# A mixer's gate projections as 2x2 block products with seven multiplications, their output products placed between the halves, and two scalings on another engine

## The chip, the cores and the metric

One core of one Trainium2 chip (trn2). The metric is the device time of one execution in microseconds (us). Three runs of the kernel before took 2802.63, 2804.25 and 2805.12 us; the median is 2804.25.

The core's engines run side by side, each through an instruction list of its own, and meet through semaphores: PE multiplies matrices (PEld is its weight load), DVE, ACT and POOL work on vectors, SP issues the transfers. PE, DVE and ACT meet in PSUM, whose banks hold what PE writes until DVE or ACT have read it; POOL works in SBUF.

## The reference, cut to what matters

A block with cross attention, a state-space mixer and a routed low-rank layer, each on a layer norm and with a residual. x has 8 sequences of 64 tokens and 512 features, 512 tokens in all; everything is fp32. The change lies in the mixer:

```python
proj = einsum('bld,pd->blp', hidden_states, in_proj_w)
gate = proj[..., :I]                       # I = 64 heads * 64 = 4096
hbc  = proj[..., I:I + CONV_DIM]           # x, B and C
dt   = proj[..., -H:]
xBC  = silu(conv over 4 tokens of hbc)
...
y  = scan(xBC, softplus(dt + dt_bias)) + x * D
yn = y * rsqrt(mean of y * y over a group of 512) * norm_weight
yn = yn * silu(gate)
out = einsum('bli,di->bld', yn, out_proj_w)
```

There are 8 groups. Each has 512 gate channels, 512 channels of x, 128 of B and 128 of C, and 8 heads of 64.

## The kernel before, in words

Cross attention takes the first 2303 us and is not touched. It and the queries already use the form of product that the change brings to the gates (`FIRST`, `SECOND` on lines 38 and 39, `weight_sums` on line 137, the queries from line 149): a matrix product is cut into 2x2 blocks, and seven block products of sums of blocks replace eight. In the queries the product is L204, its first copy and sums L220 to L225, the second half's L231 to L233, the sums of weights L141 to L144 on POOL.

`mixer_and_routed` works through the groups. Channels lie on the 128 partitions, the 512 tokens along the free axis. In a group, n counts blocks of 128 channels: n = 0 to 3 are the gates, 4 to 7 x, 8 B and 9 C. `project` (L1112 on) makes one block: four matmuls 128x512 (L1116) into a PSUM bank with the tag `pj`, of which there are three; the output products (`mo`) use the same three. For a gate ACT takes silu from PSUM into `sg` (L1122). For x, B and C, DVE does a convolution over four tokens into `acc` (L1127, then three times L1133), of which there are three buffers, and ACT takes its silu into `xbc` (L1138).

The work of a group is laid over that of its neighbours, in an order written out by hand (from L1289), within which a scheduler places the instructions of each engine by their priority and by `issue_after` (an instruction of the block isn't issued ahead of the one named). In the loop for a group `G`, with `old` the group before and `new` the one after:

- `load_out` fetches the output weights and POOL multiplies them by norm_weight (L1015); `load_in` fetches the next group's input weights; `steps` makes the next group's `av` on POOL (L1089), in four buffers.
- The convolution stretch: projections n = 8, 9, 4, 5, 6, 7, with the mixing of the old group in between: `mix` (products `pg` L1154 and transposes `px` L1165 on PE, `gm` L1158, `m` L1160 and `dx` L1167 on DVE), `scan` (16 small products per 128 tokens, L1183, added into y by DVE, L1189), and `gate` (squares on ACT L1195 and sums of them on POOL L1196 and L1198; y times sg on DVE, L1205). Then `skip`: y = x * D on POOL (L1145).
- ACT loads the table for exp and ln (L116); four sets of `decay` of the new group follow (products `seg` L1104 on PE, exp L1109 on ACT), and `norm` of the old one (`pss` L1211 on PE, then ln and exp on ACT, L1214 and L1215), which gives the factors `rs`.
- The gate stretch: gates n = 0 to 3, each followed by `project_out(old, n)`: four matmuls 128x512 (L1224), then x += product * rs on DVE (L1228).

In the last group the mixing and scans of that same group stand between its gates, and after it come its gate multiplications (L1352), `norm`, the output products and the router. Ahead of the first group stands the softplus of dt (L1035 to L1056), a chain of small instructions on DVE and ACT, on which the first decays wait.

Of the kernel before, what the change touches and what calls it, by code (L numbers as in the profile page):

```python
# [9 lines left out]
F32 = mybir.dt.float32  # L10
AF = mybir.ActivationFunctionType
ALU = mybir.AluOpType
# [3 lines left out]
P = 128  # L16
# [945 lines left out]
def mixer_and_routed(ctx, tc, c, x, done, w_in, w_out, w_ra, b_w, out):  # L962
# [43 lines left out]
    def load_out(G):  # L1006

        g = G.g
        G.wo = wst.tile([P, GC, D], F32, tag="w_out", name=f"w_out_{g}")
        nc.sync.dma_start(  # L1010
            out=G.wo, in_=w_out[g * GC * P : (g + 1) * GC * P, :].rearrange("(n p) o -> p n o", p=P)
        )
        for n in range(GC):
            ct = g * GC + n
            nc.gpsimd.tensor_scalar(G.wo[:, n, :], G.wo[:, n, :], c.nw[:, ct : ct + 1], None, op0=ALU.mult)  # L1015

# [4 lines left out]
    for tt in range(NTT):  # L1021
# [11 lines left out]
    dt = big.tile([P, NTT, H2], F32, name="dt")  # L1033
    z = big.tile([P, NTT, H2], F32, name="sp_z")
    nc.vector.tensor_tensor(z, pdt, c.dtb.unsqueeze(1).to_broadcast([P, NTT, H2]), ALU.add)  # L1035
    e = big.tile([P, NTT, H2], F32, name="sp_e")

    nc.vector.tensor_scalar(dt, z, 0.0, None, op0=ALU.max)
    nc.vector.scalar_tensor_tensor(out=e, in0=dt, scalar=-2.0, in1=z, op0=ALU.mult, op1=ALU.add)
    nc.scalar.activation(e, e, AF.Exp)  # L1040
    u = big.tile([P, NTT, H2], F32, name="sp_u")
    nc.vector.tensor_scalar(u, e, 1.0, None, op0=ALU.add)
    lu = big.tile([P, NTT, H2], F32, name="sp_lu")
    nc.scalar.activation(lu, u, AF.Ln)
# [13 lines left out]
        op0=ALU.mult, op1=ALU.mult,  # L1058
    )


# [21 lines left out]
    def steps(G, tt):  # L1083


        if tt == 0:
            G.av, G.dec = [], grpp.tile([P, NTT, HPG, S], F32, tag="dec", name="dec")
        av = wk.tile([P, 2, HH, S], F32, tag="av", name="av", bufs=4)
        nc.gpsimd.tensor_tensor(  # L1089
            av,  # L1090
            ah[:, :, tt, G.g, :].unsqueeze(3).to_broadcast([P, 2, HH, S]),
            c.upto1.unsqueeze(1).unsqueeze(1).to_broadcast([P, 2, HH, S]),
            ALU.mult,
        )
        G.av.append(av)
# [16 lines left out]
    def project(G, n):  # L1112

        pj = bank("pj", [P, NT], "pj", 3)
        for dc in range(DC):
            nc.tensor.matmul(  # L1116
                pj, lhsT=G.w[:, dc, n, :], rhs=xnT[:, dc, :], start=dc == 0, stop=dc == DC - 1
            )
        if n < GC:
            if n == 0:  # L1120
                G.sg = grpp.tile([P, GC, NT], F32, tag="sg", name="sg")
            return nc.scalar.activation(G.sg[:, n, :], pj, AF.Silu).ins  # L1122
        if n == 8:
# [8 lines left out]
        for k in range(1, KC):  # L1132
# [4 lines left out]
            )  # L1137
        return nc.scalar.activation(G.xbc[:, n - GC, :], acc, AF.Silu).ins  # L1138

    def skip(G):  # L1140

        G.y = grpp.tile([P, GC, NT], F32, tag="y", name="y")
        for n in range(GC):
            ct = G.g * GC + n
            nc.gpsimd.tensor_scalar(G.y[:, n, :], G.xbc[:, n, :], c.dk[:, ct : ct + 1], None, op0=ALU.mult)  # L1145

# [74 lines left out]
    def project_out(G, tt):  # L1221
        po = bank("pj", [P, D], "mo", 3)
        for n in range(GC):
            nc.tensor.matmul(  # L1224
                po, lhsT=G.y[:, n, tt * P : (tt + 1) * P], rhs=G.wo[:, n, :],
                start=n == 0, stop=n == GC - 1,
            )
        nc.vector.scalar_tensor_tensor(  # L1228
            out=x[:, tt, :], in0=po, scalar=G.rs[tt], in1=x[:, tt, :], op0=ALU.mult, op1=ALU.add
        )  # L1230


# [12 lines left out]
    def route(tt):  # L1245
        xnT = wk.tile([P, DC, P], F32, tag="xnT", name="rt_xnT")
        layernorm_T(nc, c, small, ps, x, tt, xnT, tag="px", bufs=2, pbufs=1, copy=nc.scalar.copy)
# [26 lines left out]
        nc.tensor.matmul(po, lhsT=whT, rhs=bw, start=True, stop=True)  # L1274
        o = wk.tile([P, D], F32, tag="o", name="o")
        nc.vector.tensor_tensor(o, x[:, tt, :], po, ALU.add)
# [4 lines left out]
    for tt in range(NTT):  # L1281
        steps(g0, tt)
    last = None
    for tt in range(NTT):
        last = decay(g0, tt)
    for g in range(G2):
# [10 lines left out]
        with tc.issue_after(last):  # L1297

            for n, behind in (
# [8 lines left out]
                if n is not None:  # L1308
                    silus.append(project(G, n))
                if old:  # L1310
                    for what, tt in behind:
                        what(old, tt)
            skip(G)
        with tc.issue_after(silus[-1]):
            table = load_ln_exp(nc).ins
        with tc.issue_after(table):
            if new:
                decay(new, 0)
                decay(new, 1)
        gates = [lambda n=n: project(G, n) for n in range(GC)]  # L1320
        if new:
# [3 lines left out]
        if old:  # L1325
            with tc.issue_after(table):
                last = norm(old, range(NTT))
        with tc.issue_after(last):
            for n in range(GC):
                if not new and n == NTT - 1:  # L1330
                    scan(G, n)
                    squares(G, n)
                last_gate = gates[n]()
                if not new:

                    for tt in ((0, 1), (2,), (3,), ())[n]:
                        mix(G, tt)
                    if 0 < n < NTT - 1:
                        scan(G, n - 1)
                        squares(G, n - 1)  # L1340
                    if n == 2:
                        scan(G, n)
                        squares(G, n)
                if old:
                    project_out(old, n)
        last = last_gate
# [79 lines left out]
```

## Time and profile before

| | us |
|---|---|
| runs | 2802.63, 2804.25, 2805.12 |
| profiled execution | 2806.07 |
| its span | 2804.40 |
| PE, DVE, ACT, POOL busy in the span | 2777.7, 1717.9, 726.3, 837.4 |
| mixer, from its first projection to its last output products | 2308.2 to 2771.6 |
| a middle group, from mixing to mixing (L1154) | 59.35 to 59.6 |
| PE's granted clock, mean | 0.998 of full speed |

How to read it: "busy" is the time in which an engine executes, without semaphores and issue. A line of the timeline gives start, length, engine, line of the kernel, operation, the tile written and those read, the shape, and how many instructions of the kind follow one another; in brackets, idle time ahead of it and what ended it. A row of the groups gives the total time, the mean in ns of one, and the engine's idle time before it with its releaser. In the last line of the page's chain, each engine has the share of the span in which the chain of work that ended last went through it.

### The profile page before, as it was taken

To read this page: it belongs to the slowest core of one execution; us is meant where nothing else is said; L and a number is where in the kernel's file an instruction comes from. 1 tells how busy PE (TensorE), PEld (TensorE's weight loads), DVE (VectorE), ACT (ScalarE), POOL (GpSimd) and SP (SyncE) were. 2 spreads that over 40 slices of the span, in tenths; PEclk is the share of its full clock that TensorE was granted. 3 is DMA by queue.
4 is the path that set the end of the run, shared out by engine and by line. 5 is a ranking of instruction groups with operands and counts; after the bars stand their busy time and mean duration, and the time that the engine had idled before them with its cause. 6 is when DMAs were issued, how large, how long until landed. Compare 5 with 4: busy or idle time off the path is not lost.

```text
span 2804.4 us, 38363 instructions
## 1 busy us (share of the span) xinstructions
PE 2777.7 (99%) x14972; PEld 1980.5 (71%) x14972; DVE 1717.9 (61%) x3044; ACT 726.3 (26%) x1314; POOL 837.4 (30%) x786
## 2 busy tenths in 40 slices
PE   9899999999999999999999999999999999999998
PEld 7677777777777777877777777778777554444444
DVE  4556676566666666765766676667656326444554
ACT  3322223222222322232222222222322103222222
POOL 4313323322222332233222223322322214333431
PEclk9999999999999999999999999999999999999999
DMA  4821322131223213221311232132212541112200
GB/s 156 276 90 46 88 67 55 53 103 44 48 54 90 54 45 89 67 55 52 103 45 48 54 89 54 48 85 67 61 31 80 168 140 38 53 53 86 72 16 15
DMA packets 277230, 206.02 MB, mean 73 GB/s; under 512 B 155676, under 2 KB 240538, under 8 KB 276026
## 3 DMA queue, kind: packets, MB, share of 16 engines
q1 hardware_dynamic: 277050, 203.57, 25.5%
q8 instruction: 119, 1.95, 0.3%
q14 instruction: 61, 0.50, 0.1%
HBM read 180.87 MB, written 22.66 MB: 73 GB/s over the span
## 4 chain that ended last, share of the span: by engine, by line
PE 87%; DVE 3%; ACT 1%; DMA 1%; issue 0%; POOL 0%; SPq 0%; ACTq 0%; DVEq 0%
PE pav L596 13%; PE psc L526 12%; PE pj L1116 8%; PE pv_a L445 6%; PE pv_b L445 6%; PE pk_b L385 6%; PE pv_c L445 6%; PE pk_c L385 6%; PE pk_a L385 5%; PE mo L1224 4%; PE pv_d L445 3%; PE pk_d L385 3%; PE psn L414 2%; DVE acc L1133 1%; PE pvl L468 1%; PE po_d L741 1%
## 5 line engine op out<-in xcount | busy, mean ns | idle before, releaser
L531 DVE SCALAR_TENSOR_TENSOR attn<-psc,rk,mask_sb 128x256 f32<-128x256 f32 (+1 forms) x832 | 364.4, 475 | 190.6 <-PE psc L526 188.8
L580 POOL TENSOR_TENSOR sm<-attn 128x512 f32<-128x512 f32 x64 | 82.0, 1281 | 1196.0 <-ACT attn L578 1196.0
L596 PE MATMUL pav<-attn,v 128*128 128x256 f32 (+1 forms) x1664 | 384.3, 381 | 0.0
L526 PE MATMUL psc<-q,kT 128*128 128x256 f32 x1536 | 367.5, 380 | 0.0
L596 PEld LDWEIGHTS pav<-attn,v 128*128 128x128 f32 (+1 forms) x1664 | 311.1, 190 | 55.4 <-issue 11.1
L583 POOL TENSOR_TENSOR sm<-sm,attn 128x512 f32<-128x512 f32 x256 | 339.9, 1328 | 28.9 <-DVE attn L574 10.6
L526 PEld LDWEIGHTS psc<-q,kT 128*128 128x128 f32 x1536 | 287.5, 190 | 77.1 <-issue 29.9
L1116 PE MATMUL pj<-mx_xnT,w_in 128*128 128x512 f32 x640 | 296.3, 603 | 1.3 <-DVE acc L1133 1.3
L574 DVE TENSOR_TENSOR attn<-attn,nb 128x1024 f32<-128x1024 f32 x192 | 224.7, 1215 | 58.1 <-ACT nb L571 57.3
L445 PEld LDWEIGHTS pv_a<-wv,cx 128*128 128x128 f32 x1536 | 196.0, 191 | 48.2 <-issue 41.4
L578 ACT ACTIVATE attn<-attn 128x1024 f32<-128x1024 f32 x192 | 203.4, 1059 | 79.8 <-DVE attn L574 77.2
L445 PE MATMUL pv_a<-wv,cx 128*128 128x128 f32 x1536 | 213.8, 279 | 0.0
L542 DVE TENSOR_TENSOR mx<-mx,attn 128x512 f32<-128x512 f32 x256 | 212.3, 829 | 2.0
L1116 PEld LDWEIGHTS pj<-mx_xnT,w_in 128*128 128x128 f32 x640 | 115.2, 190 | 129.4 <-issue 124.7
L385 PE MATMUL pk_a<-cx,wk 128*128 128x417 f32 (+1 forms) x512 | 193.3, 500 | 0.8 <-ACT qrs L110 0.8
L396 ACT ACTIVATE ksq<-kT 128x834 f32<-128x834 f32 (+1 forms) x128 | 109.2, 871 | 145.9 <-DVE kT L377 145.9
L385 PEld LDWEIGHTS pk_a<-cx,wk 128*128 128x128 f32 x512 | 97.2, 190 | 46.1 <-issue 20.8
L1228 DVE SCALAR_TENSOR_TENSOR x<-mo,rs,x 128x512 f32<-128x512 f32 x32 | 24.0, 750 | 165.1 <-PE mo L1224 110.4
L1224 PE MATMUL mo<-w_out,y 128*128 128x512 f32 x256 | 118.1, 597 | 0.0
L643 POOL TENSOR_TENSOR o<-o,f 128x512 f32<-128x512 f32 x31 | 40.0, 1291 | 232.7 <-DMA f<-sums_d 199.3
L571 ACT COPY nb<-nbs 128x256 f32<-128x256 f32 x64 | 24.1, 376 | 318.3 <-DMA nbs<-max_d 309.1
L1133 DVE SCALAR_TENSOR_TENSOR acc<-pj,small_consts,acc 128x504 f32<-128x504 f32 (+1 forms) x144 | 103.7, 724 | 0.7
(220 smaller groups left out, 4187.7 us busy)
## 6 DMA issues: line engine op xcount, KB each, us to landing
wk<-in_wk SPq DMA_DIRECT2D x32, 512.0 KB
wv<-in_wv SPq DMA_DIRECT2D x32, 512.0 KB
w_in<-in_w_in SPq DMA_DIRECT2D x16, 1024.0 KB
wvs<-wv_s_d SPq DMA_DIRECT2D x28, 512.0 KB
wks<-wk_s_d SPq DMA_DIRECT2D x28, 512.0 KB
cx<-in_ctxT SPq DMA_DIRECT2D x16, 834.0 KB
cx<-in_ctxT SPq DMA_DIRECT2D x16, 768.0 KB
wq<-in_wq SPq DMA_DIRECT2D x16, 512.0 KB
```

The lines of the kernel that those rows point to most:

```text
L385: nc.tensor.matmul(ps[:, :w], lhsT=u.wk[l][:, dc, :], rhs=u.cx.r[ch][r][:, dc, :], start=start and dc == 0, stop=dc == 1, skip_group_check ...
L445: nc.tensor.matmul(ps[:, i * HD : (i + 1) * HD], lhsT=u.cx.r[ch][r][:, dc, i * P : (i + 1) * P], rhs=u.wv[l][:, dc, :], start=start and i ...
L526: nc.tensor.matmul(ps[:rows, t - t2, :], lhsT=lhsT, rhs=qh, start=True, stop=True)
L531: nc.vector.scalar_tensor_tensor(out=s.at[:rows, t, :].rearrange("p (h q) -> p h q", h=GQ), in0=ps[:rows, t - t2, :].rearrange("p (h q) -> ...
L542: nc.vector.tensor_tensor(s.mx2, s.mx2, s.at[:, t2 : t2 + 2, :], ALU.max)
L574: nc.vector.tensor_tensor(at[:, k : k + 4, :], at[:, k : k + 4, :], nb.unsqueeze(1).to_broadcast([P, 4, 256]), ALU.add,)
L578: nc.scalar.activation(at[:, k : k + 4, :], at[:, k : k + 4, :], AF.Exp)
L583: nc.gpsimd.tensor_tensor(sm2, sm2, at[:, i : i + 2, :], ALU.add)
L596: nc.tensor.matmul(s.av[:, 0, :], lhsT=u.v[:rows, t, hh, :], rhs=s.at[:rows, t, :], start=t == 0, stop=t == NKT - 1,)
L1116: nc.tensor.matmul(pj, lhsT=G.w[:, dc, n, :], rhs=xnT[:, dc, :], start=dc == 0, stop=dc == DC - 1)
L1133: nc.vector.scalar_tensor_tensor(out=accb[:, :, k:], in0=pjb[:, :, : S - k], scalar=c.cw[:, ct, KC - 1 - k : KC - k], in1=accb[:, :, k:], ...
L1224: nc.tensor.matmul(po, lhsT=G.y[:, n, tt * P : (tt + 1) * P], rhs=G.wo[:, n, :], start=n == 0, stop=n == GC - 1,)
```

## The change

1. Gates in pairs of channel blocks (`project_gates`). A pair's product is 256 channels by 512 inputs by 512 tokens, cut in 2x2 blocks. `first` issues four block products (a, d, b, c; two matmuls 128x256 each) into two banks, of which ab holds a and b, cd holds c and d; ACT copies a (p1), DVE makes three sums. `second` issues three more products onto a, b and c, ACT takes silu of a, DVE adds b and c, and ACT takes silu of those. Output products of the old group stand after each half: first, mo0, second, mo1, first, mo2, second, mo3.
2. Sums of weights (`sums_in`, eight per group, POOL, made one group ahead) and, once, sums of tokens (`token_sums`, four 128x512 on DVE).
3. `second` comes after the factors of `norm` (`last`), `first` need not: ACT's first copy may be issued ahead of them.
4. `skip` moves from POOL to ACT, three blocks before the table load, the fourth after the factors. The weighing of the output weights (`weigh_out`) moves from POOL to ACT, after the group's last gate.
5. `behind` is issued after the projection it follows. `av` has three buffers instead of four; the softplus temporaries and two of the router's tiles take other tiles' buffers.

```diff
@@ -1010,9 +1010,19 @@
         nc.sync.dma_start(
             out=G.wo, in_=w_out[g * GC * P : (g + 1) * GC * P, :].rearrange("(n p) o -> p n o", p=P)
         )
+
+    def weigh_out(G):
         for n in range(GC):
-            ct = g * GC + n
-            nc.gpsimd.tensor_scalar(G.wo[:, n, :], G.wo[:, n, :], c.nw[:, ct : ct + 1], None, op0=ALU.mult)
+            ct = G.g * GC + n
+            nc.scalar.activation(G.wo[:, n, :], G.wo[:, n, :], AF.Copy, scale=c.nw[:, ct : ct + 1])
+
+    def sums_in(G, n):
+
+        l = {
+            f"L{k + 1}{e + 1}": G.w[:, 2 * e : 2 * e + 2, n + k, :] for k in range(2) for e in range(2)
+        }
+        G.l = getattr(G, "l", {})
+        G.l[n] = weight_sums(nc, l, wk.tile([P, 4, 2, P], F32, tag="ws", name="ws"))
 
     load_in(groups[0])
 
@@ -1031,16 +1041,17 @@
             )
 
     dt = big.tile([P, NTT, H2], F32, name="dt")
-    z = big.tile([P, NTT, H2], F32, name="sp_z")
+
+    sp = grpp.tile([P, GC, NT], F32, tag="y", name="sp")
+    z, e, u, lu = (
+        sp[:, k, : NTT * H2].rearrange("p (t h) -> p t h", h=H2) for k in range(4)
+    )
     nc.vector.tensor_tensor(z, pdt, c.dtb.unsqueeze(1).to_broadcast([P, NTT, H2]), ALU.add)
-    e = big.tile([P, NTT, H2], F32, name="sp_e")
 
     nc.vector.tensor_scalar(dt, z, 0.0, None, op0=ALU.max)
     nc.vector.scalar_tensor_tensor(out=e, in0=dt, scalar=-2.0, in1=z, op0=ALU.mult, op1=ALU.add)
     nc.scalar.activation(e, e, AF.Exp)
-    u = big.tile([P, NTT, H2], F32, name="sp_u")
     nc.vector.tensor_scalar(u, e, 1.0, None, op0=ALU.add)
-    lu = big.tile([P, NTT, H2], F32, name="sp_lu")
     nc.scalar.activation(lu, u, AF.Ln)
     nc.vector.tensor_scalar(u, u, 1.0, None, op0=ALU.subtract)
     nc.vector.tensor_scalar(z, u, 0.0, None, op0=ALU.is_equal)
@@ -1059,6 +1070,21 @@
     )
 
 
+    HT = NT // 2
+    blocks = {
+        f"R{e + 1}{half + 1}": xnT[:, 2 * e : 2 * e + 2, half * HT : (half + 1) * HT]
+        for e in range(2) for half in range(2)
+    }
+    ts = big.tile([P, 4, 2, HT], F32, name="mx_xs")
+    blocks.update((f"T{k + 1}", ts[:, k]) for k in range(4))
+
+    def token_sums():
+        for o, p, q in (
+            ("T1", "R12", "R11"), ("T2", "R22", "T1"), ("T3", "R22", "R12"), ("T4", "R21", "T2")
+        ):
+            nc.vector.tensor_tensor(blocks[o], blocks[p], blocks[q], ALU.subtract)
+
+
 
     psw = bank("seg", [P, NTT, H2], "psw", 2)
     for r in range(0, P, S):
@@ -1085,7 +1111,7 @@
 
         if tt == 0:
             G.av, G.dec = [], grpp.tile([P, NTT, HPG, S], F32, tag="dec", name="dec")
-        av = wk.tile([P, 2, HH, S], F32, tag="av", name="av", bufs=4)
+        av = wk.tile([P, 2, HH, S], F32, tag="av", name="av", bufs=3)
         nc.gpsimd.tensor_tensor(
             av,
             ah[:, :, tt, G.g, :].unsqueeze(3).to_broadcast([P, 2, HH, S]),
@@ -1113,13 +1139,9 @@
 
         pj = bank("pj", [P, NT], "pj", 3)
         for dc in range(DC):
-            nc.tensor.matmul(
+            done = nc.tensor.matmul(
                 pj, lhsT=G.w[:, dc, n, :], rhs=xnT[:, dc, :], start=dc == 0, stop=dc == DC - 1
-            )
-        if n < GC:
-            if n == 0:
-                G.sg = grpp.tile([P, GC, NT], F32, tag="sg", name="sg")
-            return nc.scalar.activation(G.sg[:, n, :], pj, AF.Silu).ins
+            ).ins
         if n == 8:
             G.xbc = grpp.tile([P, GC + 2, NT], F32, tag="xbc", name="xbc")
         ct = G.g * GC + n - GC if n < 8 else (I2 // P + G.g if n == 8 else I2 // P + G2 + G.g)
@@ -1135,14 +1157,59 @@
                 scalar=c.cw[:, ct, KC - 1 - k : KC - k], in1=accb[:, :, k:],
                 op0=ALU.mult, op1=ALU.add,
             )
-        return nc.scalar.activation(G.xbc[:, n - GC, :], acc, AF.Silu).ins
-
-    def skip(G):
-
-        G.y = grpp.tile([P, GC, NT], F32, tag="y", name="y")
-        for n in range(GC):
+        return done, nc.scalar.activation(G.xbc[:, n - GC, :], acc, AF.Silu).ins
+
+    def project_gates(G, n):
+
+
+
+        st, l = Group(), G.l[n]
+        if n == 0:
+            G.sg = grpp.tile([P, GC, NT], F32, tag="sg", name="sg")
+        to = G.sg[:, n : n + 2]
+
+        def product(k, lhs, rhs, start, stop):
+            for dc in range(2):
+                last = nc.tensor.matmul(
+                    st.ps[k], lhsT=l[lhs][:, dc, :], rhs=blocks[rhs][:, dc, :],
+                    start=start and dc == 0, stop=stop and dc == 1, skip_group_check=True,
+                ).ins
+            return last
+
+        def first():
+            st.ps = {}
+            for pair in ("ab", "cd"):
+                t = bank("pj", [P, 2, HT], f"pj_{pair}", 3)
+                st.ps[pair[0]], st.ps[pair[1]] = t[:, 0, :], t[:, 1, :]
+
+            for k, lhs, rhs in FIRST:
+                last = product(k, lhs, rhs, k in "ad", False)
+            p1 = wk.tile([P, HT], F32, tag="p1", name="p1", bufs=1)
+            nc.scalar.copy(p1, st.ps["a"])
+            st.u2 = wk.tile([P, HT], F32, tag="u2", name="u2", bufs=1)
+            nc.vector.tensor_tensor(st.u2, p1, st.ps["d"], ALU.add)
+            nc.vector.tensor_tensor(p1, st.u2, st.ps["b"], ALU.add)
+            nc.vector.tensor_tensor(to[:, 1, HT:], p1, st.ps["c"], ALU.add)
+            return last
+
+        def second():
+            for k, lhs, rhs in SECOND:
+                last = product(k, lhs, rhs, False, True)
+            nc.scalar.activation(to[:, 0, :HT], st.ps["a"], AF.Silu)
+            nc.vector.tensor_tensor(to[:, 0, HT:], st.u2, st.ps["b"], ALU.add)
+            nc.vector.tensor_tensor(to[:, 1, :HT], st.u2, st.ps["c"], ALU.add)
+            nc.scalar.activation(to[:, 0, HT:], to[:, 0, HT:], AF.Silu)
+            return last, nc.scalar.activation(to[:, 1, :], to[:, 1, :], AF.Silu).ins
+
+        return first, second
+
+    def skip(G, ns):
+
+        if ns[0] == 0:
+            G.y = grpp.tile([P, GC, NT], F32, tag="y", name="y")
+        for n in ns:
             ct = G.g * GC + n
-            nc.gpsimd.tensor_scalar(G.y[:, n, :], G.xbc[:, n, :], c.dk[:, ct : ct + 1], None, op0=ALU.mult)
+            nc.scalar.activation(G.y[:, n, :], G.xbc[:, n, :], AF.Copy, scale=c.dk[:, ct : ct + 1])
 
     def mix(G, tt):
 
@@ -1221,13 +1288,14 @@
     def project_out(G, tt):
         po = bank("pj", [P, D], "mo", 3)
         for n in range(GC):
-            nc.tensor.matmul(
+            last = nc.tensor.matmul(
                 po, lhsT=G.y[:, n, tt * P : (tt + 1) * P], rhs=G.wo[:, n, :],
                 start=n == 0, stop=n == GC - 1,
             )
         nc.vector.scalar_tensor_tensor(
             out=x[:, tt, :], in0=po, scalar=G.rs[tt], in1=x[:, tt, :], op0=ALU.mult, op1=ALU.add
         )
+        return last.ins
 
 
     w = big.tile([P, DC, E + E * R], F32, name="w_ra")
@@ -1243,7 +1311,7 @@
         nc.sync.dma_start(out=bw, in_=b_w)
 
     def route(tt):
-        xnT = wk.tile([P, DC, P], F32, tag="xnT", name="rt_xnT")
+        xnT = wk.tile([P, DC, P], F32, tag="sq", name="rt_xnT")
         layernorm_T(nc, c, small, ps, x, tt, xnT, tag="px", bufs=2, pbufs=1, copy=nc.scalar.copy)
         ph = bank("seg", [P, E + E * R], "ph", 2)
         for dc in range(DC):
@@ -1272,7 +1340,7 @@
         nc.scalar.copy(whT, pt)
         po = bank("y1", [P, D], "ro")
         nc.tensor.matmul(po, lhsT=whT, rhs=bw, start=True, stop=True)
-        o = wk.tile([P, D], F32, tag="o", name="o")
+        o = wk.tile([P, D], F32, tag="acc", name="o", bufs=3)
         nc.vector.tensor_tensor(o, x[:, tt, :], po, ALU.add)
         nc.sync.dma_start(out=out[tt * P : (tt + 1) * P, :], in_=o)
 
@@ -1280,7 +1348,7 @@
     g0 = groups[0]
     for tt in range(NTT):
         steps(g0, tt)
-    last = None
+    last = done_out = None
     for tt in range(NTT):
         last = decay(g0, tt)
     for g in range(G2):
@@ -1306,18 +1374,23 @@
                 (7, ((gate, 2), (gate, 3))),
             ):
                 if n is not None:
-                    silus.append(project(G, n))
+                    done, silu = project(G, n)
+                    silus.append(silu)
                 if old:
-                    for what, tt in behind:
-                        what(old, tt)
-            skip(G)
+                    with tc.issue_after(done if n is not None else done_out):
+                        for what, tt in behind:
+                            what(old, tt)
+            skip(G, range(GC - 1))
+        if g == 0:
+            token_sums()
+            sums_in(G, 0)
+            sums_in(G, 2)
         with tc.issue_after(silus[-1]):
             table = load_ln_exp(nc).ins
         with tc.issue_after(table):
             if new:
                 decay(new, 0)
                 decay(new, 1)
-        gates = [lambda n=n: project(G, n) for n in range(GC)]
         if new:
             with tc.issue_after(table):
                 last2 = decay(new, 2)
@@ -1325,24 +1398,44 @@
         if old:
             with tc.issue_after(table):
                 last = norm(old, range(NTT))
+
+        def own(*what):
+
+            if not new:
+                for step, tt in what:
+                    step(G, tt)
+
         with tc.issue_after(last):
-            for n in range(GC):
-                if not new and n == NTT - 1:
-                    scan(G, n)
-                    squares(G, n)
-                last_gate = gates[n]()
-                if not new:
-
-                    for tt in ((0, 1), (2,), (3,), ())[n]:
-                        mix(G, tt)
-                    if 0 < n < NTT - 1:
-                        scan(G, n - 1)
-                        squares(G, n - 1)
-                    if n == 2:
-                        scan(G, n)
-                        squares(G, n)
-                if old:
-                    project_out(old, n)
+            skip(G, [GC - 1])
+
+
+        done_out = None
+        for k in range(2):
+            first, second = project_gates(G, 2 * k)
+            if k:
+                own((scan, 3), (squares, 3))
+            with tc.issue_after(done_out) if k else nullcontext():
+                done_out = first()
+            if not k:
+                own((mix, 0), (mix, 1))
+            if old:
+                with tc.issue_after(done_out):
+                    done_out = project_out(old, 2 * k)
+            if not k:
+                own((scan, 0), (squares, 0), (mix, 2))
+            with tc.issue_after(done_out), tc.issue_after(last):
+                done_out, last_gate = second()
+            if not k:
+                own((scan, 1), (squares, 1), (mix, 3))
+            if old:
+                with tc.issue_after(done_out):
+                    done_out = project_out(old, 2 * k + 1)
+            if not k:
+                own((scan, 2), (squares, 2))
+            if new:
+                sums_in(new, 2 * k)
+        with tc.issue_after(last_gate):
+            weigh_out(G)
         last = last_gate
 
     G = groups[-1]
```

## The prediction

> **What bounds the kernel now.** I read the page's first part and its chain first, then a table of PE's busy time over windows of 70 us, then the timelines of DVE, PE and POOL around one group's gates. Two lines of the page:
>
> ```profile
> PE 2777.7 (99%) x14972; PEld 1980.5 (71%) x14972; DVE 1717.9 (61%) x3044; ACT 726.3 (26%) x1314; POOL 837.4 (30%) x786
> ...
> PE 87%; DVE 3%; ACT 1%; DMA 1%; issue 0%; POOL 0%; SPq 0%; ACTq 0%; DVEq 0%
> ```
>
> TensorE is busy throughout. The mixer, which the change is confined to, runs from 2308.2 to 2771.6 us (then come the last output products and the router, to 2804.4). The table of windows has PE busy for
>
> ```profile
> 2390.00:2460.00 70.00, 69.79 (x347) 32.37 (x344) 32.62 (x54) 17.75 (x33) 24.25 (x21) 1.00 0.16 53
> 2460.00:2530.00 70.00, 69.79 (x341) 31.61 (x339) 32.28 (x54) 15.46 (x28) 22.98 (x20) 1.00 0.19 63
> ```
>
> (window, length, then busy time of PE, PEld, DVE, ACT, POOL, the clock, DMA share and GB/s): 69.8 of 70. PE time taken away is time gained, unless the engines that are now hidden come out. So I look at how late each is. Below, every time marked + counts from a group's first decay product (L1104); for the group shown it stands at 2378.94. First PE, then DVE, then POOL:
>
> ```profile
> 2378.94 0.66 PE L1104 MATMUL seg<-av,past 64*64 64x256 f32 x8
> 2379.53 3.70 PE L1116 MATMUL pj<-mx_xnT,w_in 128*128 128x512 f32 x8
> 2383.07 2.74 PE L1224 MATMUL mo<-w_out,y 128*128 128x512 f32 x6
> 2386.02 0.84 PE L1104 MATMUL seg<-av,past 64*64 64x256 f32 x8 [0.21 <-ACT dec L1109]
> ```
>
> ```profile
> 2379.80 1.53 DVE L1205 TENSOR_TENSOR y<-y,sg 128x512 f32<-128x512 f32 x1
> 2381.26 2.26 DVE L1133 SCALAR_TENSOR_TENSOR acc<-pj,small_consts,acc 128x504 f32<-128x504 f32 x3
> 2392.56 0.75 DVE L1228 SCALAR_TENSOR_TENSOR x<-mo,rs,x 128x512 f32<-128x512 f32 x1 [9.05 <-ACT rs L1215]
> ```
>
> ```profile
> 2379.74 1.04 POOL L1089 TENSOR_TENSOR av<-ah,upto 128x512 f32<-128x512 f32 x1
> ```
>
> DVE is behind PE here: the convolution of the group's last projection (n=7) ends at 2383.52, +4.57. From the next group's mixing to that point DVE is busy some 24 of 27 us, so this lag is real. One part of it is visible: the gate L1205 takes 1.53 because POOL's `av` starts just ahead of it; the same instruction alone takes 0.67 to 0.68. A group lasts 59.35 to 59.6 us, and from + 0 to the next mixing product (L1154) 31.97.
>
> **Part 1, the gates' products.** Removed: per pair of column blocks two projections of four matmuls 128x512. A projection (eight records, since an fp32 matmul shows as two) holds PE for 3.43 us, so a pair costs 6.87. Added: seven block products of two matmuls 128x256. Their price is in the queries, which have the same form:
>
> ```profile
> 67.12 1.03 PE L204 MATMUL pq_ab<-xnT,wq 128*128 128x256 f32 x4
> 67.98 1.03 PE L204 MATMUL pq_ab<-xnT,wqs 128*128 128x256 f32 x4
> 68.85 1.03 PE L204 MATMUL pq_cd<-xs,wq 128*128 128x256 f32 x4
> ```
>
> Their starts are 0.866 apart, so seven take 6.06: 0.81 less per pair, 1.62 per group, 12.9 over eight. A record of 256 columns thus starts every 0.216, with a weight load (PEld) of 0.19 beside it.
> [...]
>
> **Part 2, which waits show.** Output products now all use one PSUM bank in a steady group (by the listing of each engine's order in the changed kernel), the one that n=7's projection has just left. mo0 therefore waits for n=7's last convolution step. The first four block products end at +4.16; DVE at +4.57, plus 0.05 of release and 0.1 of restart: mo0 starts at +4.72 and PE loses about 0.5. mo1 waits for x<-mo0, which needs `rs` from the sums of squares (L1211): in the trace x starts 1.51 after those products and lasts 0.75. They move to +12.34 (earlier pieces 0.59 for a decay set, 0.866 for a product), so mo1 starts at 14.75 instead of about 14.1: 0.65 lost. The rest follows without a wait: first half of the second pair to 21.65, mo2 to 25.08, second half to 27.68, mo3 to 31.11, the next mixing at 31.2. Before: 31.97. A steady group gains 0.78, and groups 1 to 5 gain **3.9**.
>
> In group 6 there is no `av` ahead of the gate before the change (its convolution ends at +3.69, the stretch is 31.52 long); with three `av` buffers the fourth `av` waits for this group's decay, so the collision comes here too. I take a gain of **0.35**.
>
> Group 7 has no next group: its 37.08 from the end of n=7 to the last output products lose 1.62 of products, 0.3 because the sums of squares no longer stand behind POOL's skip, and about 0.4 in switches between shapes: **2.3**.
>
> Group 0 loses. Four token sums of 128x512 (0.68 each by the gate's row, 2.7) stand in DVE's softplus chain; two idle gaps of 0.48 there (DVE waiting for ACT) hide 1.0, so all behind it comes 1.7 later: decays, table load, `xbc`, and through the `acc` buffers n=5's convolution, for which PE waited 1.29 before, now about 3. Then the second half waits 0.9 for the first copy's sums, and the next group's first projection 0.9 for the bank that L1199 empties behind ACT's silus and their table load (1.28). Against this 1.62 is saved: **-1.9**.
>
> **Part 3, the rest.** DVE gets ten adds 128x256 per group (0.42 each by L222 to L233, 4.2), all in the gate stretch, where it is busy 6.7 of 32 us. POOL loses 105.3 us and gets 64 weight sums (47 at 0.73), also there:
>
> ```profile
> L1145 POOL TENSOR_SCALAR y<-xbc,small_consts 128x512 f32<-128x512 f32 x32 | 55.8, 1745 | 50.1 <-ACT xbc L1138 50.1
> L1015 POOL TENSOR_SCALAR w_out<-w_out,small_consts 128x512 f32<-128x512 f32 x32 | 49.5, 1567 | 179.9 <-DMA w_out<-in_w_out 177.3 <-DMA spare<-in_wo 2.6
> ```
>
> ACT takes over both: 64 scalings at about 0.6 (its 128x512 silu from PSUM is 0.596), 38 us. Three skips stand between the `xbc` silus; ACT is busy 5 of 27 us there, so I cost them at nothing; if one pushes a square and so a gate of the old group, that is up to 0.6 per group. The weighing of w_out is behind the last silu, with the third and fourth output products as cover. No new DMA; SP's order is unchanged. The tail (32.8) stays.
>
> **Sum:** 3.9 + 0.35 + 2.3 - 1.9 = 4.65. The profiled execution took 2806.07 (span 2804.40 and 1.67 around it), so it becomes 2801.4; it lies 1.8 above the median of the runs, 2804.25, on which the forecast is **2799.6**. The bounds of each term: a steady group between 0 and 1.62+0.35 (its present small waits) gained, group 0 between -3.5 and 0, group 7 between 1.6 and 2.9.
>
> **Rivals.** A, *the waits don't show*: POOL's skip is gone, `av` moves, the convolution ends at +3.7 as in group 6, and mo0 waits for nothing; 0.5 to 1.0 more in six groups and part of group 0: 2793 to 2796. For it: group 6's row. Against: `av` still comes at the decay.
> B, *the saving is eaten*: the two waits are a little longer (another 0.5 each) or group 0 loses 3.5: 2802 to 2806.
> C, *DVE becomes the bound*: the place is mo0, behind n=7's convolution. From +4.16 on, each microsecond that DVE is later costs one in each of groups 1 to 6. One collision like the shown gate costs 0.85; DVE has eight instructions per group with two SBUF operands (`m` and gates), and POOL's weight sums and ACT's skips are new beside them. The gain is gone at 4.65/6 = 0.8 later per group, one collision; two more give 10.2 - 4.65 = 5.5 slower, 2810. Against it: POOL's work in the convolution stretch falls, and the weight sums are placed after the gates.
> [...]
> That the change does not do what it says is excluded: the order listing has 14 products of 128x256 per pair.
>
> **Chances and range.** Forecast (2796.5 to 2802.5) 0.45, A 0.2, B 0.2, C 0.15. Leaving out the far end of A and of C, the range is 2793 to 2809. A measurement of this kernel can tell about 0.2%, 5.6 us, from no change, so faster is below 2798.6 and slower above 2809.9. Faster: A and somewhat under half of the forecast, 0.39; slower: two thirds of C, 0.1; the same: 0.51.
>
> **What would show it.** Right: block products at 0.866 each; in a steady group mo0 waiting for a DVE convolution and mo1 for x, each near half a microsecond; 31.2 from the first decay to the mixing; group 0 with a wait of about 3 us ahead of its gates. Wrong: a convolution of n=7 ending past +5.5, an `m` or gate at 1.5 in more places, block products above 0.9, or DVE idle less than 1 us in the convolution stretch.

## The result and the profile after

The changed kernel takes 2800.53 us (median of 20 runs, 2798.30 to 2801.99), the kernel before 2804.32 (20 runs): ratio 0.9985, 95% interval 0.9978 to 0.9991. That is 3.8 us less, forecast were 4.65 less; it is faster, by less than the 0.2% that the prediction set as its bound for "faster", and lies inside its forecast (2796.5 to 2802.5). The profiled execution has a span of 2799.9.

The page after the change, its first part and the chain of what ended last:

```profile
PE 2766.0 (99%) x15164; PEld 2014.8 (72%) x15164; DVE 1754.0 (63%) x3128; ACT 776.6 (28%) x1410; POOL 778.7 (28%) x786
...
PE 89%; DVE 2%; DMA 1%; ACT 0%; issue 0%; SPq 0%; ACTq 0%; DVEq 0%
```

PE lost 11.7 us of busy time and is still the bound; DVE gained 36, ACT 50, POOL lost 59. The rest shows in the table of PE's waits (time, times, longest), of which these lines lie in the mixer:

```profile
PE pj_ab L1173 <- DVE acc L1155: 3.3, 1, 3.3
PE mo L1291 <- DVE x L1295: 2.4, 6, 0.4
...
PE mo L1291 <- issue: 1.5, 4, 0.4
...
PE pj_ab L1173 <- DVE p L1191: 1.1, 1, 1.1
PE mo L1291 <- DVE acc L1155: 0.8, 2, 0.4
...
PE pj L1142 <- DVE sg L1199: 0.3, 1, 0.3
```

Before, the mixer had one wait of 1.3 and five of 0.2. The third line belongs to the fifth: mo0 waits 0.4 in each of groups 1 to 6, in four of them put down to "issue". In the timeline of group 1 (its first decay product at 2382.23) mo0 and mo1 stand so:

```profile
2385.52 1.03 PE L1173 MATMUL pj_cd<-mx_xs,ws 128*128 128x256 f32 x4
2386.95 2.81 PE L1291 MATMUL mo<-w_out,y 128*128 128x512 f32 x6 [0.41 <-DVE acc L1155]
...
2396.89 3.70 PE L1291 MATMUL mo<-w_out,y 128*128 128x512 f32 x8 [0.41 <-DVE x L1295]
...
2413.43 0.34 PE L1221 MATMUL pg<-xbc 128*64 128x64 f32 x4
```

Cause and place are those of the prediction. Its 0.5 and 0.65 are time lost by PE, restarts and delayed starts included, not the idle time in the brackets; e10 below, which has neither wait, is the measure for them. mo0 starts 0.15 after the convolution's end (2386.95 against 2384.54 + 2.26, DVE's line under e4), the 0.05 and 0.1 of the prediction together. Counted from 2382.23, mo0 starts at +4.72 and mo1 at +14.66, where +4.72 and +14.75 were forecast. From decay to mixing are 31.20, as forecast.

The whole of the mixer, read from the first projection, the first decay product (seg) and the first mixing product (pg) of each group in the two timelines:

| stretch | before | after | gain | forecast |
|---|---|---|---|---|
| group 0: first projection to the first seg in group 1's stretch | 70.73 | 74.20 | -3.47 | -1.9 |
| seg to pg, groups 1 to 5, sum | 159.88 | 155.84 | 4.04 | 3.9 |
| seg to pg, group 6 | 31.52 | 31.15 | 0.37 | 0.35 |
| pg to seg, groups 2 to 6, sum | 136.97 | 136.51 | 0.46 | 0 |
| group 7, pg to the last output products | 64.30 | 61.20 | 3.10 | 2.3 |
| ahead of the mixer, and behind it | | | 0.18 - 0.18 | 0 |
| sum | | | 4.50 | 4.65 |

That the sum of the profiles is so near the forecast is partly luck: group 0 is 1.6 worse, group 7 is 0.8 and the mixing stretches (pg to seg) are 0.46 better than forecast. The start of the mixer, behind a stage that both kernels share, lies between 2304.86 and 2308.21 in the profiles of this study. So spans of single profiles are not compared below, only stretches counted from that start; and totals as medians.

**Group 0** holds what the prediction did not see. PE's timeline, and PE's granted clock in a table of windows (start:end, length, busy times, then the clock ahead of the last two columns):

```profile
2336.65 1.13 PE L1173 MATMUL pj_ab<-mx_xnT,w_in 128*128 128x256 f32 x4 [3.27 <-DVE acc L1155]
2337.62 1.81 PE L1173 MATMUL pj_cd<-mx_xs,ws 128*128 128x256 f32 x4
2339.22 1.91 PE L1173 MATMUL pj_ab<-mx_xs,ws 128*128 128x256 f32 x4
2340.93 1.13 PE L1173 MATMUL pj_cd<-mx_xs,ws 128*128 128x256 f32 x4
2343.19 1.10 PE L1173 MATMUL pj_ab<-mx_xnT,w_in 128*128 128x256 f32 x4 [1.13 <-DVE p L1191]
```

```profile
2336.00:2337.00 1.00, 0.35 (x2) 0.32 (x3) 1.00 (x2) 0.37 (x1) 0.00 (x0) 1.00 0.00 0
...
2338.00:2339.00 1.00, 1.00 (x4) 0.82 (x3) 0.96 (x2) 0.97 (x3) 0.00 (x0) 0.50 0.00 0
2339.00:2340.00 1.00, 1.00 (x4) 0.81 (x3) 0.96 (x2) 0.29 (x1) 0.00 (x0) 0.50 0.00 0
2340.00:2341.00 1.00, 1.00 (x4) 0.74 (x3) 0.26 (x1) 0.00 (x0) 0.00 (x0) 0.50 0.00 0
```

After the wait of 3.27 the second and third block product take 1.60 and 1.71 where 0.866 is usual, and the clock is 0.50.

### The profile page after: what moved, and what is told of

It reads as the page before. It is cut to its first block, busy times and chain, and to the rows that moved or that the text cites. A ratio compares the mean times of both kernels' runs of the same rounds, so it can differ in the third digit from the quotient of the medians.

```text
span 2799.9 us, 38952 instructions
## 1 busy us (share of the span) xinstructions
PE 2766.0 (99%) x15164; PEld 2014.8 (72%) x15164; DVE 1754.0 (63%) x3128; ACT 776.6 (28%) x1410; POOL 778.7 (28%) x786
## 4 chain that ended last, share of the span: by engine, by line
PE 89%; DVE 2%; DMA 1%; ACT 0%; issue 0%; SPq 0%; ACTq 0%; DVEq 0%
PE pav L596 13%; PE psc L526 12%; PE pv_a L445 6%; PE pj L1142 6%; PE pv_b L445 6%; PE pk_b L385 6%; PE pv_c L445 6%; PE pk_c L385 6%; PE pk_a L385 5%; PE mo L1291 4%; PE pv_d L445 3%; PE pk_d L385 3%; PE pj_ab L1173 2%; PE psn L414 2%; PE pj_cd L1173 1%; PE pvl L468 1%
## 5 line engine op out<-in xcount | busy, mean ns | idle before, releaser
L1142 PE MATMUL pj<-mx_xnT,w_in 128*128 128x512 f32 x384 | 176.4, 602 | 0.3 <-DVE sg L1199 0.3
L1142 PEld LDWEIGHTS pj<-mx_xnT,w_in 128*128 128x128 f32 x384 | 69.0, 190 | 72.9 <-issue 70.3
L375 ACT COPY kT<-pk_a 128x384 f32<-128x384 f32 x64 | 31.6, 494 | 265.5 <-PE pk_a L385 265.4
```

The source lines that it names most:

```text
L1142: done = nc.tensor.matmul(pj, lhsT=G.w[:, dc, n, :], rhs=xnT[:, dc, :], start=dc == 0, stop=dc == DC - 1).ins
```

## The experiments

**Theory.** The block products cost what the rows of the queries say; groups 1 to 6 lose exactly two waits for a bank (mo0, mo1); group 0 loses 1.7 us by the token sums in the softplus chain, and up to 1.7 by a half clock that follows PE's wait. **Rivals:** the slow products come from their operands; group 0 is late by ACT's skips; DVE is the bound, and a wait that is taken away comes back elsewhere. Except for e8, each kernel is the changed one with the edit shown. Every median stands beside the 2800.5 of the changed kernel, each ratio is to the kernel before, which was timed again beside each set of runs (medians 2804.63 to 2805.36).

**e1_sums_late**

```diff
-            (nc.vector.tensor_copy if b == half else nc.scalar.copy)(
+            copied = (nc.vector.tensor_copy if b == half else nc.scalar.copy)(
...
         if g == 0:
-            token_sums()
+            with tc.issue_after(copied.ins):
+                token_sums()
```

> The four token sums are put behind the copies that follow the softplus chain; all else is the changed kernel. My theory: in group 0 the sums delay the chain by 1.6 us, this lengthens PE's wait ahead of the first block product to 3.3 us, and after that wait the granted clock is at half for some 3 us (the block products take 1.6 to 1.7 us where 0.87 is usual). So with the sums out of the chain the wait falls to about 1.6 us, the clock stays at 1.0, and the time falls by about 3.2 us, to 2797.3 on the median. Rival 1, the sums are hidden and group 0 is late for another reason (ACT's skips among the silus): no change, within 0.5 us. Rival 2, the slow products come from their operands (sums just written), not from the wait: only 1.6 us less, and the products still take 1.6 us.

2795.53 us, ratio 0.9971 (0.9959 to 0.9982). Group 0's stretch is 70.79, 3.41 less, and the same as before the change (70.73).

```profile
2331.76 1.13 PE L1173 MATMUL pj_ab<-mx_xnT,w_in 128*128 128x256 f32 x4 [1.54 <-DVE acc L1155]
2332.73 1.03 PE L1173 MATMUL pj_cd<-mx_xs,ws 128*128 128x256 f32 x4
2333.59 1.03 PE L1173 MATMUL pj_ab<-mx_xs,ws 128*128 128x256 f32 x4
2334.45 1.03 PE L1173 MATMUL pj_cd<-mx_xs,ws 128*128 128x256 f32 x4
```

The wait falls from 3.27 to 1.54, so the sums cost 1.73; the products are 0.87 apart with the same operands. Rivals 1 and 2 of this run fall. The median is 5.0 below that of the changed kernel, more than the 3.41 of the stretch; the rest is not accounted for, and single runs of either kernel spread over 3 to 4 us.

**e2_g0_warm**

```diff
         done_out = None
+        if g == 0:
+            wm = bank("y0", [P, NT], "wm")
+            for i in range(3):
+                done_out = nc.tensor.matmul(wm, lhsT=c.ident, rhs=xnT[:, 0, :], start=True, stop=True).ins
         for k in range(2):
...
-            with tc.issue_after(done_out) if k else nullcontext():
+            with tc.issue_after(done_out) if k or g == 0 else nullcontext():
```

> Three extra matmuls 128x512 (0.86 us each, result unused) stand in PE's order ahead of group 0's first block product, inside the wait of 3.3 us; everything else is the changed kernel. Theory (half clock because PE was idle): the wait's end is unchanged, the clock stays at 1.0, the first four block products take 0.87 us each instead of 0.97 to 1.7, and up to 1.7 us are gained; since the next products wait for DVE's sums of the first copy (1.13 us now), part of it may go into that wait: 1 to 1.7 us less, 2799.2 on the median. Rival (slow because of operands or of DVE's and ACT's accesses beside them): no gain, the products still take 1.6 us.

2798.72 us, ratio 0.9980 (0.9971 to 0.9988). Group 0's stretch is 72.51, 1.69 less than 74.20. The sums still delay it; only the clock is different:

```profile
2332.15 2.84 PE L1416 MATMUL wm<-mx_xnT,ident 128*128 128x512 f32 x6
2335.49 1.13 PE L1173 MATMUL pj_ab<-mx_xnT,w_in 128*128 128x256 f32 x4 [0.49 <-DVE acc L1155]
2336.45 1.03 PE L1173 MATMUL pj_cd<-mx_xs,ws 128*128 128x256 f32 x4
```

So the half clock costs 1.69 when it comes. It does not always come: of six profiles with the wait of 3.26 or 3.27, four have it (after, e4, e6, e7) and two, with the same instructions in group 0, have not (e3 and e9, both 72.51). Group 0's loss is therefore 1.78 or 3.47, from one execution to the next. For the same reason e2's single profile does not show by itself that the extra products keep the half clock away. That the operands are not the cause is shown by e3 and e9: the same products after the same wait are 0.86 to 0.87 apart there, at a clock of 1.00.

**e3_mo_banks**

```diff
-    def project_out(G, tt):
-        po = bank("pj", [P, D], "mo", 3)
+    def project_out(G, tt, own=False):
+        po = bank(f"y{tt % 2}", [P, D], "mo") if own else bank("pj", [P, D], "mo", 3)
...
-                    done_out = project_out(old, 2 * k)
+                    done_out = project_out(old, 2 * k, bool(new))
...
-                    done_out = project_out(old, 2 * k + 1)
+                    done_out = project_out(old, 2 * k + 1, bool(new))
```

> The old group's output products take the two PSUM banks of the scans (idle in the gate stretch) in turn, instead of a bank shared with the projections; the instructions and their order are unchanged. Theory: mo0's wait for n=7's convolution (0.41) and mo1's for x (0.41) are waits for the bank alone, both vanish in groups 1 to 6, 12 x 0.41 = 4.9 us less, 2795.6 on the median. Rival (DVE is the bound and the lateness only moves): the waits come back as waits of second's products or of the next projections for DVE, and the gain is below 2 us.

2795.56 us, ratio 0.9969 (0.9957 to 0.9981), 5.0 less. Seg to pg is 30.30 in groups 1 to 6, both waits are gone from the table of waits and no other has come into it. The two waits were waits for a bank, worth 0.85 to 0.9 per group by this edit, and 31.98 - 30.30 = 1.68 is what the stretch gains without them (forecast for the products alone: 1.62). The rival (DVE as the bound) falls for this size, but a small part of the lateness does come back: the decay products, which follow ACT and so n=7's convolution, are held up a little, as e10 shows.

**e4_av_late**

```diff
-            for tt in range(NTT):
+            for tt in range(NTT - 1 if old else NTT):
                 steps(new, tt)
...
+        if behind:
+            with tc.issue_after(behind):
+                nc.vector.memset(av[:, 0, 0, 0:1], 0.0)
...
+        if new and old:
+            steps(new, NTT - 1, old.gated)
```

(`old.gated` is the instruction of the group's last gate, L1272.)

> POOL's fourth av of a group is made to wait for the old group's last gate multiplication, by a one-column write of DVE into its buffer behind that multiplication; all else is the changed kernel. Theory: the gate takes 0.68 instead of 1.55 us, n=7's convolution ends about 0.8 us earlier, mo0's wait of 0.41 vanishes in groups 1 to 6: 2.5 us less, 2798.0. mo1's wait stays at 0.4 us, because the sums of squares move with mo0. Rival: the gate's length is not POOL's doing, it stays at 1.5 us and nothing changes.

2796.40 us, ratio 0.9973 (0.9962 to 0.9984), 4.1 less. DVE around the gate in the changed kernel, and with the edit:

```profile
2383.07 1.55 DVE L1272 TENSOR_TENSOR y<-y,sg 128x512 f32<-128x512 f32 x1
2384.54 2.26 DVE L1155 SCALAR_TENSOR_TENSOR acc<-pj,small_consts,acc 128x504 f32<-128x504 f32 x3
```

```profile
2379.95 0.68 DVE L1275 TENSOR_TENSOR y<-y,sg 128x512 f32<-128x512 f32 x1
```

The gate is short, mo0's wait is gone, mo1's 0.41 stays, as expected; seg to pg is 30.55. That is 0.6 less, not 0.41. A likely reason is that the restart goes with the wait (the first six records of mo0 take 2.81 behind it, 2.74 with the edit) and that the decay products also follow n=7's convolution through ACT; no run takes the two apart.

**e5_sums_and_banks**: the edits of e1 and e3 together.

> Both edits together on the changed kernel: token sums behind the softplus chain, output products in the scans' banks. Theory: the two losses lie in different places (group 0, and groups 1 to 6), so the gains add: by the profiles 1.7 for the sums, 0 or 1.7 for the half clock that the longer wait brings in some executions, and 0.87 in each of six groups, 5.2; together 7 to 9 less than the changed kernel's 2800.5, 2792 to 2793.5. From one first decay product to the next mixing 30.30 in groups 1 to 6, from the first projection to group 1's first decay 70.8. Rival: once PE is faster DVE's lateness comes out elsewhere (next projections waiting for a convolution), the gain stays at about 5.

2791.95 us, ratio 0.9954 (0.9941 to 0.9966), 8.6 less. Group 0 is 70.80, seg to pg 30.30: the gains add.

**e6_dve_late**

```diff
+        if n == 7:
+            nc.vector.tensor_tensor(acc, acc, acc, ALU.max)
         accb = acc.rearrange("p (b t) -> p b t", b=B)
```

> One DVE instruction 128x512 (the maximum of the convolution's buffer with itself, about 0.68 us) is added to n=7's convolution in every group, otherwise the changed kernel. Rival C of the prediction holds that from the end of the first half each microsecond of DVE's lateness at this place costs one in each of groups 1 to 6: the wait of mo0 grows from 0.41 to about 1.1, 6 x 0.68 = 4.1 us slower, and about as much again can come in groups 0 and 7 (0.7 each): 2804.6 to 2806. If the lateness were taken up elsewhere (by mo1's wait, which then shrinks), it would cost less than 2 us.

2806.97 us, ratio 1.0007 (0.9998 to 1.0016), 6.4 more than the changed kernel. Seg to pg is 31.87 to 31.93, 0.72 more in each of six groups; group 0 is 1.37 longer, group 7 0.74. mo0's wait is 1.1. Rival C's price holds, one microsecond per microsecond (0.72 for an instruction forecast at 0.68), and one such instruction eats the gain of the change; what did not happen in the changed kernel is the lateness itself.

**e7_copy_behind**

```diff
-        def first():
+        def first(after=None):
...
-            nc.scalar.copy(p1, st.ps["a"])
+            with tc.issue_after(after) if after else nullcontext():
+                nc.scalar.copy(p1, st.ps["a"])
...
-                done_out = first()
+                done_out = first(None if k else last)
```

> Only the third part of the change undone: ACT's first copy of a group stands behind the factors of norm, as silus did before. Theory: the second half's first product waits for the copy's sums; the scheduler then puts the sums of squares ahead of it, PE has nothing between the decay products, which are paced by ACT at 1.65 us, and after them waits about 2.6 us for factors, skip, copy and two sums: 3.5 to 4 us per group in groups 1 to 6 and a few in group 0: 2822 to 2828, slower than the kernel before. Rival: the copy is off the path, because another product could fill the wait: less than 3 us in all.

2837.36 us, ratio 1.0115 (1.0101 to 1.0129): slower, and by more than expected.

```profile
2397.14 1.05 PE L1279 MATMUL pss<-ones,s 128*128 128x1 f32 x8 [0.48 <-ACT dec L1135]
2400.66 2.05 PE L1173 MATMUL pj_ab<-mx_xnT,w_in 128*128 128x256 f32 x4 [2.46 <-DVE p L1192]
2402.49 1.91 PE L1173 MATMUL pj_ab<-mx_xnT,ws 128*128 128x256 f32 x4
2404.20 1.91 PE L1173 MATMUL pj_cd<-mx_xs,w_in 128*128 128x256 f32 x4
```

The waits are those expected (0.58, 0.48 and 2.46 in group 1). The half clock comes on top: products 1.7 apart, 0.50 in the windows from 2400 to 2406. Each of the six groups has a product of 2.04 or 2.05 where 1.03 to 1.13 is usual, and group 0 two such stretches (up to 2.08 and up to 1.91). Seg to pg is 35.69 to 37.30. Without the early copy (point 3 of the change) the block products are a loss.

**e8_scal_only**: the kernel before, with `skip` and `weigh_out` on ACT.

```diff
-            nc.gpsimd.tensor_scalar(G.wo[:, n, :], G.wo[:, n, :], c.nw[:, ct : ct + 1], None, op0=ALU.mult)
+            nc.scalar.activation(G.wo[:, n, :], G.wo[:, n, :], AF.Copy, scale=c.nw[:, ct : ct + 1])
...
-            nc.gpsimd.tensor_scalar(G.y[:, n, :], G.xbc[:, n, :], c.dk[:, ct : ct + 1], None, op0=ALU.mult)
+            nc.scalar.activation(G.y[:, n, :], G.xbc[:, n, :], AF.Copy, scale=c.dk[:, ct : ct + 1])
```

> The kernel before, with only the two scalings moved from POOL to ACT (three skips between the silus, the fourth behind the factors, the weighing of w_out behind the last gate); gates, buffers and order as before. By my reading these moves are worth little by themselves: the convolution stretch is shorter by 0.47 in all after the change, and group 7's sums of squares come 0.3 earlier: 0.5 to 1 us less than before, 2803.5. Rival 1: POOL's long instructions slowed DVE enough that most of group 7's and the steady groups' gain came from here: 2 us or more. Rival 2: ACT's extra instructions delay squares and gates: slower by 1 to 3 us.

2803.76 us, ratio 0.9996 (0.9988 to 1.0005): no difference that the times can tell. The stretches can: pg to seg is 27.30 in groups 2 to 6 where it was 27.30 to 27.57, group 7 is 0.27 shorter, group 0 0.21 longer. So the 0.46 of the table comes from the scalings.

**e9_out_after**

```diff
-            if old:
-                with tc.issue_after(done_out):
-                    done_out = project_out(old, 2 * k)
...
             if old:
-                with tc.issue_after(done_out):
-                    done_out = project_out(old, 2 * k + 1)
+                for tt in (2 * k, 2 * k + 1):
+                    with tc.issue_after(done_out):
+                        done_out = project_out(old, tt)
```

> Only the second part of the change undone: both output products stand behind a pair's second half. Theory: in the first pair the second half's first product waits for the first copy's sums behind n=7's convolution (about 1.4 us after the first half), the decay products then wait for ACT (0.6), while mo0's and mo1's waits of 0.41 vanish; the second pair waits about 0.2: 0.6 us per group more than the changed kernel, 3 to 5 us in all, 2803.5 to 2805.5, so the block products without this order would gain nothing against the kernel before. Rival: PE has enough other pieces (decay products, sums of squares) to fill the wait: within 1 us of the changed kernel.

2815.99 us, ratio 1.0044 (1.0031 to 1.0058): 15.5 more than the changed kernel, three to five times the 3 to 5 that I expected. The places of the output products, which this run undoes, are in point 1 of the change. The second pair:

```profile
2461.28 1.03 PE L1173 MATMUL pj_cd<-mx_xs,ws 128*128 128x256 f32 x4
2463.42 1.10 PE L1173 MATMUL pj_ab<-mx_xnT,w_in 128*128 128x256 f32 x4 [1.11 <-DVE p L1191]
```

```profile
2462.40 0.42 DVE L1190 TENSOR_TENSOR u<-p,pj_cd 128x256 f32<-128x256 f32 x1 [2.76 <-PE pj_cd L1173]
2462.86 0.42 DVE L1191 TENSOR_TENSOR p<-u,pj_ab 128x256 f32<-128x256 f32 x1
```

I had let the first sum (L1190) start when product d was there. It starts when c is, the last of the four. c and d lie in one tile and one bank; which of the two makes the sum wait, no run tests. The two sums are then all in the open, 1.11 to 1.19 in each pair. Seg to pg is 33.37 in five of the groups, 2.2 more than after the change. In the sixth, group 3, it is 34.95:

```profile
2505.86 1.10 PE L1173 MATMUL pj_ab<-mx_xnT,w_in 128*128 128x256 f32 x4 [1.19 <-DVE p L1191]
2507.37 1.33 PE L1130 MATMUL seg<-av,past 64*64 64x256 f32 x8 [0.42 <-issue]
2508.64 2.07 PE L1173 MATMUL pj_ab<-mx_xnT,ws 128*128 128x256 f32 x4
```

The waits are those of the other groups, but what follows them is slow: the decay set takes 1.33 and the block product 2.07, where group 2 has 0.88 and 1.13 behind the same waits. By these lengths (2.05 and 1.91 at the clock of 0.50 in e7) the half clock is here too, and it costs 1.58. So it does not take a wait of 3 us.

**e10_all**: the edits of e1, e3 and e4 together.

> Token sums behind the chain, output products in the scans' banks, and the fourth av behind the gate. The two edits of the run before leave one wait in a middle group, a decay product 0.2 us for ACT, which follows n=7's convolution; with the gate no longer held up it goes: 30.30 becomes about 30.1, 6 x 0.2 = 1.2 us less than with two edits, 2790.7. Rival: the two waits were the whole of what the gate cost, and nothing more comes: 2792, 30.30.

2788.91 us, ratio 0.9943 (0.9931 to 0.9956), 11.6 less than the changed kernel and the fastest of this study. Seg to pg is 29.87 in all six groups, less than the 30.1 expected; in the middle groups no wait of PE is left in the table. What remains there of the mixer are group 0's two, 1.5 and 1.1, and 0.3 ahead of the next projection. In group 2 (its first decay product at 2433.95):

```profile
2438.10 2.74 PE L1294 MATMUL mo<-w_out,y 128*128 128x512 f32 x6
...
2447.38 3.60 PE L1294 MATMUL mo<-w_out,y 128*128 128x512 f32 x8
```

mo0 starts at +4.15 and mo1 at +13.43. Against the changed kernel's +4.72 and +14.66 that is 0.57 for the first wait and 0.66 more for the second: the 0.5 and 0.65 of the prediction. With the banks alone (e3) the stretch is 0.43 longer than here, so part of what the gate costs is not in the two waits but in the decay products behind n=7's convolution; the rival falls.

## Why the prediction was right, and where it was not

- **Part 1, the products.** 0.866 for four records of 256 columns, from the queries' rows: measured 0.86 to 0.87 in the changed kernel. 1.62 per group: 1.68 once the waits are gone (e3).
- **Part 2, steady groups.** Right in cause, place and size: 31.20 forecast and measured, 0.37 in group 6 against 0.35. The later pieces start where they were forecast too (mo2 at +21.65, mo3 at +27.67). e3 took both waits away, e4 the first alone, e10 both with what caused the first; by e10's starts they cost 0.57 and 0.66, as forecast. Not all of this price comes back with the banks alone: 0.85 to 0.9 of it did (e3).
- **Group 0.** The delay by the token sums was sized right (1.7; e1: 1.73), and without the half clock the whole term is -1.78 (forecast -1.9). The second wait was 1.13 instead of 0.9, that of the next projection 0.30 instead of 0.9. The half clock is missing from the prediction: 1.69 in the profile, in two thirds of the profiles with this wait. The prediction had "about 3" for the wait and did not ask what the clock does behind it.
 The half clock stands for 3.4 us in group 0 (3.42 after the change and in e4, 3.40 in e6 and e7, from the clocks of the windows) and for 6.84 in group 1 of e7 (0.28 + 6 + 0.56, windows of two microseconds from 2398 on), and the same wait does and does not bring it: one of 3.26 or 3.27 is followed by 0.50 in four of six profiles. Shorter waits were followed by it too: 0.58, 0.48 and 2.46 with products between them in e7, and, by the lengths of the products, 1.19 and 0.42 in group 3 of e9. Group 0's waits of 1.54 or 1.55 (e1, e5, e10) and of 0.49 (e2) were not followed by it, in one profile each. How much idle time brings it stays open.
- **Group 7** was mis-sized: 2.3 forecast, 3.10 measured. Of it, 1.62 is products and 0.27 the scalings (e8; forecast 0.3). The remaining 1.2 against my 0.4 is left over by subtraction; in the timelines the scans cut the output products into fewer pieces after the change, but no run measured this by itself.
- **Part 3.** ACT's scalings were costed at nothing and gain 0.46 and 0.27 and cost 0.21 in group 0 (e8); by which wait they gain, no run shows. The ten sums on DVE and POOL's weight sums found idle time, as forecast.
- **Rivals.** A asked for the waits not to show; they do. B's price, group 0 losing 3.5, came true in the profile, but group 7 and the mixing stretches made up for most of it. C's mechanism is there with the price named (e6), and the change stays short of it by one instruction.
- What the prediction left unsaid is that two other parts of the change make the block products pay: without the places of the output products between the halves the changed kernel is 11 us slower than the kernel before (e9), without the early copy 32 (e7).

## What to carry to other kernels

PE, busy 99% of the span, gave back what was taken from it only where the results were fetched in time (3.8 us with the two waits for a bank, 5.0 more without them, e3): price the split of a product by its sums' way back (copy, first sum, second sum, and which bank each shares; with the two sums in the open a pair waited 1.11 to 1.19, e9), and put other products of about that length between the halves. Before anything else, ask which bank or buffer an inserted piece waits for; here two idle banks and later places for the token sums and for one `av` were worth three times the change itself (11.6 us against 3.8). Count stretches from a common mark, since the stages ahead of it moved by 3 us from one execution to the next (the mixer starts between 2304.86 and 2308.21).

## What the hardware showed

- TensorE's granted clock stood at one half after a wait of 3.27 us, for about 3.4 us (after the change the windows of one microsecond from 2337 on have 0.86, 0.50, 0.50, 0.50 and 0.93, so 0.28 + 3 + 0.14), starting about 1 us after PE resumed at 2336.65, and in four of six profiles with this wait. In e7 it started 0.4 us before PE resumed at 2335.29 (0.72 in the window from 2334 to 2336, so 1.12 of it).
- In group 1 of e7 it started 0.9 us before PE resumed at 2400.66 (0.93 in the window from 2398 to 2400, so 0.28 of it).
- Scaling 128x512 on ACT with a factor per partition took 0.72 for `skip` (L1212) and 2.55 for four of w_out (L1017) in the changed kernel, where POOL took 1.745 (L1145) and 1.567 (L1015) each before.
- DVE's gate multiplication of 128x512 (L1272, two SBUF operands) took 1.55 with POOL's `av` beside it in the changed kernel and 0.68 where that `av` was made to wait for it (e4).
